# Attention columns from turned weights, adjacency loaded once, and exponentials turned by VectorE in a four-layer graph network

## The chip, the core and the metric

The kernel runs on one core of one Trainium2 chip. The metric is device time in microseconds (us) of the whole kernel. A core has five engines with queues of their own: TensorE (PE, matrix products and transposes into PSUM), VectorE (DVE), ScalarE (ACT), GpSimd (POOL) and SyncE (SP, which here only issues transfers). Transfers run on 16 DMA engines whatever queue issued them.

## The reference

128 graphs of 64 nodes with 256 features pass four layers. Each layer normalises its input, applies ReLU, and adds the layer's output to the input. `adj` is 128x64x64, integers 0 or 1.

```python
# layer 0: four heads (h) of 64 features (f)
Wh = (X @ W).reshape(B, N, H, F)
e_src = einsum('bnhf,hf->bnh', Wh, a_src)
e_dst = einsum('bjhf,hf->bjh', Wh, a_dst)
e = leaky_relu(e_src[:, :, None, :] + e_dst[:, None, :, :], 0.2)
alpha = softmax(where(A > 0, e, -1e9), axis=2)
out = elu(einsum('bijh,bjhf->bihf', alpha, Wh))
# layer 1: the same with one head; its vectors are a[:256] and a[256:]
# layer 2: relu(sum over relations r of (adj == r) @ ((x W + b_r) * sigmoid(x W Wg + bg_r)))
# layer 3: three steps of a GRU cell on aggr = A^T (h weight[i]) and h
```

Since `adj` holds 0 and 1 alone, of layer 2 only the relation 1 contributes. A flag computed on the chip sends other data to a general path, which these inputs don't take.

## The kernel before

**Tiling.** Two graphs fill the 128 partitions (a pair); four pairs are a group `g`, so there are 16 groups. Each group passes three layers of attention and relation and then three GRU steps. Everything is float32.

**Order.** The kernel body doesn't issue instructions; it notes them. `Plan.note` records each with its engine, an estimated cost, what it writes and reads, and the job it belongs to. `Plan.emit` (its last lines are around 525) then runs a list scheduler over the notes: `forward` places each instruction by an estimate of when its inputs, its engine and its buffers are free, `backward` derives due times from that, this is repeated `PASSES` times from a seed, and then a list of seeds `MOVES` shifts the due times of whole jobs. The order with which it ends is the order on every queue. Costs come from the function `cost` (line 575 and after): a transfer has a rate in bytes per ns by the tag of the tile that it fills. So a changed cost, an added instruction or another seed can reorder all five queues.

**Fillers.** In the first 115 us of that estimate, where TensorE is expected to idle, `emit` puts in products of a tile of ones, `warm` (line 1638), one for each 220 ns of the expected gap over 100 ns. Nobody reads their result.

**The first weights.** `attention_columns` appends to the weights `w0e` (256x256, held as 128x2x256) the columns W a_src and W a_dst of each head, so that one product gives Wh, e_src and e_dst together. VectorE makes them: `a_src` and `a_dst` are loaded onto all 128 partitions (`AB`), multiplied into the weights (`wa`) and summed by head. The same is done for `w1e`.

**Adjacency.** `load_group` loads `at`, integers, with four transfers of 32 KB; `edge_bounds` makes of it the bounds `m` (a huge number at an edge, a tiny one elsewhere, 0 in rows that have an edge and 1e-24 in rows that have none), turns them on TensorE into `mt`, and keeps the largest entry in `amax` for the flag. `load_edges` loads the same numbers as `ag` for the GRU, with another transfer, and as `eg`, turned otherwise, for layer 2. `before` (through `before_recurrence`) makes the 0/1 matrix `abd` out of `ag`.

**Exponentials.** `attention` writes the softmax's numerators without the sum of e_src and e_dst: exp(leaky(s+d)), divided by a factor of the row, is max(exp(d), exp(0.2 d) * exp(-0.8 s)). `fd` and `gd` are exp of the d half of `es`, per partition. exp(-0.8 s) has to lie along the free dimension, the same in all 64 partitions of a graph. For groups 0 and 1 (`g < AHEAD`) TensorE does that with a diagonal; for the 14 others ScalarE makes `fs`, TensorE transposes it, VectorE copies it out of PSUM to `fT`, one transfer writes it to DRAM (`row`) and two read it back into `t`, broadcast to 64 partitions each. Then three VectorE passes (`gd`, `fd`, `mt`) finish `t`, and 64x64 products on halves of the array (`aggregate_graphs`, line 841) use it.

**GRU.** `Recurrence.step` forms its matrix products in seven parts each (`sy`, `sz`). They are most of TensorE's instructions. Its transposes between steps go through DRAM (`tb`, `way`, `hnat`).

Almost all instructions carry line 549, that of the recording helper, so the profile tells them apart by the tiles' names.

Of the kernel before, what the change touches and what calls it, by code (L numbers as in the profile page):

```python
# [10 lines left out]
F32 = mybir.dt.float32  # L11
I32 = mybir.dt.int32
# [5 lines left out]
S = 32  # L18
# [9 lines left out]
NEG1 = -9000000000000000.0  # L28
ALPHA = 0.2
EPS = 1e-5  # L30
BIG, TINY = 3.0e38, 1.0e-24
BOUND = 6.25
NREL = 39
RC = 5
# [188 lines left out]
class Plan:  # L223
# [30 lines left out]
    def note(self, engine, call, cost, writes, reads, after=(), port=0.0, dma=False):  # L254
# [23 lines left out]
            b.ops.append(op)  # L278
        return op

    PASSES, SEED, SPREAD = 27, 39, 50.0
    MOVES = (
        10, 12, 18, 24, 27, 28, 58, 71, 83, 84, 89, 99, 118, 129, 136, 141, 144, 198, 214, 221, 266, 299, 322, 324,
        334, 341, 346, 390, 400, 412, 424, 434, 550, 559, 579, 611, 616, 682, 785, 808, 825, 869, 910, 1123, 1323,
        1710, 1729, 1754, 1784, 1908, 1924, 1933, 2133, 2158, 2174, 2755, 2883, 3921, 3988, 4026, 4270, 4596, 4876,
        4885, 5049, 5501, 5547, 5750, 5954, 6055, 6156, 6434, 6590, 7283, 7340, 7414, 7540, 7602, 7657, 7774, 7857,
        7930, 7942, 8201, 8457, 8683, 8685, 9083, 9436, 9811, 9967, 10320, 10820, 10999, 11484, 11701, 12627, 12696,
        12718, 12783, 12858, 12980, 13024, 13178, 13347, 13474, 14022, 14057, 14422, 14846, 16253, 16751, 16786,
        17194, 18227, 19571, 21611, 22526, 22951, 22990, 23107, 24055, 25299,
    )  # L290
    LEEWAY = {"PE": 100.0, "DVE": 100.0, "Activation": 100.0, "Pool": 100.0, "SP": 300.0, "-": 0.0}
    OVERLAP = {"DVE": 83.0, "Activation": 95.0, "Pool": 43.0}
# [210 lines left out]
    def emit(self):  # L503

        self.on = False
        self.link()
        best, self.random = None, Random(self.SEED)
        for _ in range(self.PASSES):
            ranks = [op.due for op in self.ops]
            end, order = self.forward()  # L510
            if best is None or end < best[0]:
                best = end, ranks, [op.start for op in self.ops]
            self.backward(end)
        end, ranks, starts = best
        jobs = list({id(op.job): op.job for op in self.ops}.values())
        for j in jobs:
            j.sum, j.count, j.shift = 0.0, 0, dict.fromkeys(self.RANKED, 0.0)
        for op, start in zip(self.ops, starts):
            op.job.sum, op.job.count = op.job.sum + start, op.job.count + 1
        for m in self.MOVES:  # L520
            self.move(m, end, jobs)
        for op, due in zip(self.ops, ranks):
            op.due = due + op.job.shift.get(op.engine, 0.0)
        end, order = self.forward()
        best = end, [(op, op.start, op.idle, op.places) for op in order]
        self.ends = best[0]
        for op, start, idle, places in best[1]:
            op.start = start
            if op.engine == "PE" and self.spare and start < 115.0 * 1e3:
                for _ in range(int((idle - 100.0) / 220.0)):  # L530
                    self.spare()
            for b, tag in places:
                b.pool.make(b, tag)
            op.call()
        self.ops = []
        return best[0]
# [46 lines left out]
def cost(engine, method, args, kwargs):  # L583
# [4 lines left out]
        return (m / 1.2 + 2.5) * (1 if method == "transpose" else 2)  # L588
    if engine == "sync" or method == "dma_start":
        to, of = args[:2]  # L590
        rate = {"way": 450.0, "fine": 220.0}.get(to.base.tag, 150.0) if isinstance(to, View) else 150.0
        if isinstance(of, View) and of.base.tag in ("way", "fine"):
            rate = 170.0 if of.base.tag == "way" else 125.0
        return n * to.shape[0] * 4 / rate
# [15 lines left out]
def kernel(  # L610
# [33 lines left out]
    xr = x.rearrange("b n d -> (b n) d").rearrange("(t q) d -> q t d", q=P)  # L644
    ar = adj.rearrange("b n m -> (b n) m").rearrange("(t q) m -> q t m", q=P)

    tr = adj.rearrange("(t r a) i j -> t a i r j", r=2, a=2)
    er = adj.rearrange("(t r a) j i -> t r j a i", r=2, a=2)
    outr = out.rearrange("b n d -> (b n) d").rearrange("(t q) d -> q t d", q=P)

# [7 lines left out]

    same = nc.kept(const, [P, P], F32, name="same")
    diag = nc.kept(const, [P, N], F32, name="diag")  # L660
    amax = nc.kept(const, [P, NG], F32, name="amax")
    flag = nc.kept(const, [1, 1], I32, name="flag")
    wc = nc.kept(const, [P, LAYERS, K, 3 * D], F32, name="wc")
    whh = nc.kept(const, [P, K, 3 * D], F32, name="whh")
# [554 lines left out]
    with ExitStack() as s1:  # L1219
# [47 lines left out]
        class Layer:  # L1267
# [2 lines left out]

            place = {"em": "hn", "dg": "hn", "tb": "hn", "land": "hn"}

            shared = {"hn": 3, "o": 2, "st": 4, "mv": 4, "var": 4, "rstd": 4, "nm": 4, "rec": 4, "fT": 1}

            def __init__(self, layer, pool, bufs):
                self.layer, self.pool, self.bufs = layer, pool, bufs
# [12 lines left out]
        W = [Layer(0, work, {"es": 2, "fd": 2, "gd": 2}), Layer(1, work, {}), Layer(2, work, {"u": 2})]  # L1289

        nc.begin("loads")
        AB = work.tile([P, 4, D], F32, name="AB", tag="o", bufs=2)
        for i, a in enumerate((a_src, a_dst)):
            nc.scalar.dma_start(AB[:, i, :], over_partitions(a, D))
        nc.scalar.dma_start(w0e[:, :, :D], rows(W0))
        AT, XG, AG, EG = [], [], [], []

        def load_group(g):
            nc.begin(("load", g))
            xg = work.tile([P, G, D], F32, name="xg", bufs=5)  # L1300
            n = 2 if g == 0 else G
            for p in range(0, G, n):
                nc.sync.dma_start(xg[:, p : p + n], xr[:, g * G + p : g * G + p + n, :])
            at = work.tile([P, G // 2, 2, N], I32, name="at", bufs=3)
            for a in range(2):
                for u in range(G // 2):
                    edges = tr[g * G // 2 + u, a]
                    nc.sync.dma_start(at[a * N : (a + 1) * N, u], edges)
            AT.append(at)
            XG.append(xg)  # L1310

        def load_edges(g):
            ag = work.tile([P, G, N], I32, name="ag", bufs=4)
            nc.sync.dma_start(ag, ar[:, g * G : (g + 1) * G, :])
            AG.append(ag)
            eg = work.tile([P, G, N], I32, name="eg", bufs=2)
            for r in range(2):
                for u in range(G // 2):
                    nc.sync.dma_start(eg[r * N : (r + 1) * N, 2 * u : 2 * u + 2], er[g * G // 2 + u, r])
            EG.append(eg)  # L1320
# [5 lines left out]
        load_group(1)  # L1326
        nc.begin("more loads")
        nc.sync.dma_start(w1e[:, :, :D], rows(W1))
        for i, a in enumerate((a1[:D], a1[D:])):
            nc.sync.dma_start(AB[:, 2 + i, :], over_partitions(a, D))  # L1330
        wn, gn = loaded(early, "wn", W_loop), loaded(early, "gn", Wg_loop)
        ihn, hhn = loaded(early, "ihn", w_ih), loaded(early, "hhn", w_hh)
        for i, b in enumerate((b_loop, bg_loop)):
# [16 lines left out]
        nc.vector.memset(mhalf, -0.5)  # L1350
        nc.vector.memset(eps, EPS)

        def attention_columns(w, heads, pieces):

            for i, ab in enumerate(pieces):
                wa = work.tile([P, K, D], F32, name="wa", tag="hn", bufs=3)
                nc.vector.tensor_tensor(wa, w[:, :, :D], ab[:, None, :].to_broadcast([P, K, D]), ALU.mult)
                nc.vector.tensor_reduce(
                    w[:, :, D + i * heads : D + (i + 1) * heads],
                    wa.rearrange("p k (h f) -> p k h f", h=heads), AX.X, ALU.add,  # L1360
                )

        wl = once.tile([P, K, 2 * D], F32, name="wl")

        def edge_bounds(g):


            at = AT[g]
            top = work.tile([P, G // 2, 2], F32, name="top")
            nc.vector.tensor_reduce(top, at, AX.X, ALU.max)  # L1370
            nc.vector.tensor_reduce(amax[:, g : g + 1], top, AX.XY, ALU.max)
            nc.vector.tensor_scalar(top, top, 0.0, TINY, op0=ALU.is_le, op1=ALU.mult)
            m = work.tile([P, G // 2, 2, N], F32, name="m", bufs=1)
            nc.vector.tensor_scalar(m, at, 0.0, BIG, op0=ALU.is_gt, op1=ALU.mult)
            nc.vector.tensor_tensor(m, m, top[:, :, :, None].to_broadcast([P, G // 2, 2, N]), ALU.max)
            pt = psum.tile([P, T], F32, name="tp")
            for u in range(G // 2):
                nc.tensor.transpose(pt[:, u * P : (u + 1) * P], m[:, u].rearrange("p g j -> p (g j)"), ident)
# [4 lines left out]
        def attention(g, p0, n, layer, heads, we, pool):  # L1383
# [31 lines left out]
                    )  # L1415
            else:

                fs = pool.tile([P, n, heads], F32, name="fs")
                nc.scalar.activation(fs, es[:, :, :heads], AF.Exp, scale=ALPHA - 1.0)
                pt = psum.tile([P, T], F32, name="tp")  # L1420
                nc.tensor.transpose(pt[:nh, :P], fs.rearrange("p g h -> p (g h)"), ident)
                fT = pool.tile([nh, P], F32, name="fT")
                nc.vector.tensor_copy(fT, pt[:nh, :P])
                row = dram.tile([2, nh * N], F32, name=f"row{layer}")
                nc.sync.dma_start(row.rearrange("a (c i) -> c a i", i=N), fT.rearrange("c (a i) -> c a i", i=N))
                for half in range(2):
                    nc.sync.dma_start(
                        t[half * N : (half + 1) * N].rearrange("p c i -> p (c i)"),
                        row[half : half + 1, :].to_broadcast([N, nh * N]),
                    )  # L1430
            flat = lambda d, c: d.rearrange("p g h -> p (g h)")[:, c, None].to_broadcast([P, len(range(nh)[c]), N])
            m = 2 if heads > 1 else n
# [8 lines left out]
            elu_add(pool, src, o, nc.vector if g < 1 else nc.gpsimd, g >= AHEAD)  # L1441

        def first_weights():
            attention_columns(w0e, H, (AB[:, 0, :], AB[:, 1, :]))
            attention_columns(w1e, 1, (AB[:, 2, :], AB[:, 3, :]))

        def later_weights(prep):
            relational_weights(prep, psum, wl, wn, gn, 0.5)
# [79 lines left out]
        def before(g):  # L1528
            ABD[g] = work.tile([P, G, N], F32, name="abd")
            by_dma = dram if g >= AHEAD else None  # L1530
            START[g] = before_recurrence(W[3], psum, XG[g], AG[g], ABD[g], by_dma, g in PLAIN)

        def recur(g):
            return Recurrence(
# [321 lines left out]
```

## Time and profile before

| | us |
|---|---|
| median of 3 runs | 1317.81 |
| lowest, highest | 1317.18, 1320.26 |
| profiled execution | 1316.05 |
| its span, first to last instruction | 1314.2 |
| granted TensorE clock | 0.998 |

The page gives for each engine its busy time, its share of the span and its instructions; then 40 slices of the span; then the DMA queues, the chain of work that ended last, the costliest groups and the transfers. On TensorE a matrix product of float32 appears as two records, a transpose as one, and their ends are modelled. Its chain of work goes through TensorE for 85% of the span:

```profile
PE 85%; DVE 5%; ACT 5%; POOL 2%; issue 1%; DMA 1%; SPq 0%; ACTq 0%; DVEq 0%; POOLq 0%
```

Transfers that the change touches, with KB each and the median us from issue to landing:

```profile
t<-row SPq DMA_DIRECT2D x28, 256.0 KB, 4.1
at<-in_adj_dram SPq DMA_DIRECT2D x64, 32.0 KB, 2.5
...
ag<-in_adj_dram SPq DMA_DIRECT2D x16, 128.0 KB, 2.8
t<-row SPq DMA_DIRECT2D x28, 64.0 KB, 2.6
```

### The profile page before, as it was taken

The page shows a single profiled execution, that of the slowest core. Times are in us where ns is not written, and L with a number is a line of the kernel's source. Part 1 is how long each engine was busy: PE and PEld are TensorE (multiplying, and loading weights), DVE is VectorE, ACT ScalarE, POOL GpSimd, SP SyncE. Part 2 cuts the span into 40 slices and gives each one's busy share as a digit, 9 for nine tenths or more (in the row PEclk, how much of TensorE's full clock was granted, in tenths as well). Part 3 has the DMA queues.
Part 4 walks back from the last instruction along what each step waited for, and adds up shares of the span by engine and source line. Part 5 has one row for each costly group of instructions (what it writes and reads, how often), then busy time and mean ns, then how long its engine had stood idle before and what let it go on. Part 6 is the DMA issues. An engine that isn't in the chain of part 4 may idle for free.

```text
span 1314.2 us, 27889 instructions
## 1 busy us (share of the span) xinstructions
PE 1298.9 (99%) x9837; PEld 1030.0 (78%) x9837; DVE 1058.3 (81%) x2562; ACT 856.6 (65%) x2173; POOL 694.3 (53%) x845
## 2 busy tenths in 40 slices
PE   9999999999999999999999999999999999999997
PEld 8667887878787777878778787877878788778885
DVE  6878667978879798897968889796887979786666
ACT  5867765666776676667766666776666667645543
POOL 2745744646555545546535564654556447445453
PEclk9999999999999999999999999999999999999999
DMA  7232122335334343443434344334334423142222
GB/s 229 66 101 58 53 85 89 110 121 161 110 117 143 115 138 94 144 122 116 126 118 142 92 150 120 104 122 132 113 104 143 132 86 129 38 129 65 65 65 68
DMA packets 132782, 144.94 MB, mean 110 GB/s; under 512 B 43417, under 2 KB 117913, under 8 KB 132633
## 3 DMA queue, kind: packets, MB, share of 16 engines
q1 hardware_dynamic: 132072, 142.54, 35.8%
q8 instruction: 80, 1.31, 0.4%
q10 hardware_dynamic: 560, 0.52, 0.1%
q14 instruction: 70, 0.57, 0.1%
HBM read 81.01 MB, written 61.49 MB: 108 GB/s over the span
## 4 chain that ended last, share of the span: by engine, by line
PE 85%; DVE 5%; ACT 5%; POOL 2%; issue 1%; DMA 1%; SPq 0%; ACTq 0%; DVEq 0%; POOLq 0%
PE sy L549 34%; PE sz L549 25%; PE mm L549 15%; PE mm L841 3%; PE tp L841 3%; ACT hn L549 2%; DVE hT L549 2%; PE sz L1638 1%; PE tp L549 1%; DVE t L549 1%; ACT hT L549 1%; PE tq L841 1%; DVE r L549 1%; POOL rstd L549 1%; DVE st L549 1%
## 5 line engine op out<-in xcount | busy, mean ns | idle before, releaser
L549 POOL TENSOR_TENSOR r<-hT,hT 128x256 f32<-128x256 f32 x192 | 156.2, 820 | 274.9 <-ACT hT L549 273.6
L549 DVE SCALAR_TENSOR_TENSOR hT<-r,hT 128x256 f32<-128x256 f32 (+1 forms) x290 | 182.4, 633 | 26.8 <-ACT r L549 24.5
L549 PE MATMUL sy<-hS,wsum 128*128 128x256 f32 x576 | 172.4, 383 | 1.2 <-ACT r L549 0.7
L549 PE MATMUL sy<-aS,wsum 128*128 128x256 f32 x576 | 172.4, 382 | 0.0
L549 PE MATMUL sz<-hS,whh 128*128 128x256 f32 x576 | 171.4, 383 | 0.6 <-DVE z L549 0.6
L549 PE MATMUL sz<-aS,wc 128*128 128x256 f32 x576 | 167.0, 383 | 0.8 <-DVE hT L549 0.8
L549 DVE TENSOR_TENSOR hT<-hT,sz 128x256 f32<-128x256 f32 x288 | 118.2, 410 | 39.5 <-PE sz L549 32.9
L549 ACT ACTIVATE hT<-hT,bi 128x256 f32<-128x256 f32 x192 | 95.7, 505 | 61.9 <-DVE hT L549 60.8
L549 POOL TENSOR_TENSOR aS<-aT 128x256 f32<-128x256 f32 x96 | 82.5, 859 | 94.0 <-ACT aT L549 94.0
L549 PEld LDWEIGHTS sy<-hS,wsum 128*128 128x128 f32 x576 | 106.8, 190 | 30.4 <-issue 9.4
L549 PEld LDWEIGHTS sy<-aS,wsum 128*128 128x128 f32 x576 | 107.6, 190 | 21.1 <-issue 4.2
L549 PEld LDWEIGHTS sz<-hS,whh 128*128 128x128 f32 x576 | 106.4, 190 | 22.4 <-issue 5.2
L549 PEld LDWEIGHTS sz<-aS,wc 128*128 128x128 f32 x576 | 106.9, 190 | 17.8 <-DVE hT L549 1.2
L549 ACT ACTIVATE hn<-xg,nm,rstd 128x256 f32<-128x256 f32 x200 | 108.0, 592 | 19.6 <-POOL nm L549 18.3
L549 ACT ACTIVATE hT<-sy,bh 128x256 f32<-128x256 f32 x192 | 90.2, 470 | 45.6 <-PE sy L549 42.4
L549 POOL TENSOR_TENSOR rstd<-var,mhalf 128x4 f32<-128x4 f32 (+1 forms) x70 | 78.1, 1115 | 77.0 <-ACT var L549 76.8
L549 PE MATMUL mm<-wl,hT 128*128 128x512 f32 x248 | 118.6, 594 | 0.0
L549 ACT COPY z<-sy 128x256 f32<-128x256 f32 x192 | 70.4, 367 | 64.9 <-PE sy L549 63.7
L549 DVE TENSOR_TENSOR hT<-hT,sy 128x256 f32<-128x256 f32 x192 | 79.3, 413 | 36.3 <-PE sy L549 34.1
L549 DVE BATCH_NORM_STATS2 st<-xg 128x6 f32<-128x256 f32 x256 | 96.3, 408 | 8.2 <-POOL xg L549 4.8
L549 DVE TENSOR_TENSOR z<-sz,z 128x256 f32<-128x256 f32 x192 | 79.5, 415 | 28.7 <-PE sz L549 27.2
L549 POOL TENSOR_TENSOR hS<-hT 128x256 f32<-128x256 f32 x96 | 80.0, 834 | 38.1 <-DMA hT<-way 15.2
(207 smaller groups left out, 3212.6 us busy)
## 6 DMA issues: line engine op xcount, KB each, us to landing
way<-tb SPq DMA_DIRECT2D x59, 512.0 KB, 2.7
hnat<-way SPq DMA_DIRECT2D x184, 128.0 KB, 3.0
way<-hn SPq DMA_DIRECT2D x42, 512.0 KB, 3.0
hn<-way SPq DMA_DIRECT2D x168, 128.0 KB, 3.1
xg<-in_x_dram SPq DMA_DIRECT2D x15, 512.0 KB, 4.4
out_dram<-xg SPq DMA_DIRECT2D x15, 512.0 KB, 2.9
t<-row SPq DMA_DIRECT2D x28, 256.0 KB, 4.1
hT<-way SPq DMA_DIRECT2D x52, 128.0 KB, 2.8
```

Of the source, the lines that this page charges most:

```text
L549: return do(*[real(a) for a in args], **{k: real(v) for k, v in kwargs.items()})
L841: nc.nc.tensor.matmul(*[real(x) for x in product], start=True, stop=True)
L1638: nc.spare = lambda: psum.spare and nc.nc.tensor.matmul(pause, warm, warm, start=True, stop=True)
```

## The change

1. **Attention columns on TensorE.** The vectors are loaded element by element onto partitions as `ab` (three transfers on ACT's queue, behind `w0e`). VectorE places them in a block-diagonal `e0` (and `e1`), TensorE transposes the weights (4 transposes each), ScalarE copies them to `wT`, TensorE multiplies `wT` with `e0`, and ScalarE copies the result into the weights' last columns. The multiplications and reductions on VectorE go.
2. **Adjacency once.** `at` is one transfer for each group, in six buffers, and serves `edge_bounds` and `abd`; `ag` goes. In `edge_bounds` one `scalar_tensor_tensor` takes the place of two passes, and `amax` keeps each row's largest entry directly (64 columns instead of 16). The huge number becomes 1e29.
3. **Exponentials turned by VectorE.** For the 14 later groups `fs` is 128x32, exp(-0.8 x) of both halves of `es` (in layer 1 eight columns, GpSimd clears the rest once a group); VectorE turns its four blocks of 32x32 in place; four transfers, one for each block, write them to `row`; two read the s half of it into `t`, in runs of one pair instead of one run.
4. **The listing.** Rates of transfers in `cost` (190 for `t`, 290 for most loads, was 150), 40 passes, another seed and other moves, and in the first 12 us of the estimate a filler for each 280 ns of a gap instead of 220.

```diff
-    PASSES, SEED, SPREAD = 27, 39, 50.0
+    PASSES, SEED, SPREAD = 40, 35, 50.0
...
-                for _ in range(int((idle - 100.0) / 220.0)):
+                for _ in range(int((idle - 100.0) / (280.0 if start < 12e3 else 220.0))):
                     self.spare()
...
-        rate = {"way": 450.0, "fine": 220.0}.get(to.base.tag, 150.0) if isinstance(to, View) else 150.0
+        tag = to.base.tag if isinstance(to, View) else None
+        rate = {"way": 450.0, "fine": 220.0, "t0": 190.0, "t1": 190.0}.get(tag, 150.0 if tag in (None, "at", "eg", "o", "row0", "row1") else 290.0)
...
-            at = work.tile([P, G // 2, 2, N], I32, name="at", bufs=3)
-            for a in range(2):
-                for u in range(G // 2):
-                    edges = tr[g * G // 2 + u, a]
-                    nc.sync.dma_start(at[a * N : (a + 1) * N, u], edges)
+            at = work.tile([P, G, N], I32, name="at", bufs=6)
+            nc.sync.dma_start(at, ar[:, g * G : (g + 1) * G, :])
...
-            ag = work.tile([P, G, N], I32, name="ag", bufs=4)
-            nc.sync.dma_start(ag, ar[:, g * G : (g + 1) * G, :])
...
-        def attention_columns(w, heads, pieces):
-            for i, ab in enumerate(pieces):
-                wa = work.tile([P, K, D], F32, name="wa", tag="hn", bufs=3)
-                nc.vector.tensor_tensor(wa, w[:, :, :D], ab[:, None, :].to_broadcast([P, K, D]), ALU.mult)
-                nc.vector.tensor_reduce(
-                    w[:, :, D + i * heads : D + (i + 1) * heads],
-                    wa.rearrange("p k (h f) -> p k h f", h=heads), AX.X, ALU.add,
-                )
+        def attention_columns(w, heads, ends):
+            wT = work.tile([P, K, D], F32, name="wT", tag="hn", bufs=3)
+            for c in range(K):
+                pt = psum.tile([P, T], F32, name="tp")
+                for k in range(K):
+                    nc.tensor.transpose(pt[:, k * P : (k + 1) * P], w[:, k, c * P : (c + 1) * P], ident)
+                nc.scalar.copy(wT[:, c], pt[:, :D])
+            n = 2 * heads
+            pm = psum.tile([P, K, n], F32, name="mm")
+            def products():
+                for k in range(K):
+                    for c in range(K):
+                        nc.nc.tensor.matmul(
+                            real(pm)[:, k], real(wT)[:, c, k * P : (k + 1) * P], real(ends)[:, c, :n],
+                            start=(c == 0), stop=(c == K - 1),
+                        )
+            nc.note("PE", products, 880.0, [pm], [wT, ends])
+            nc.scalar.copy(w[:, :, D:], pm)
...
-            nc.vector.tensor_scalar(m, at, 0.0, BIG, op0=ALU.is_gt, op1=ALU.mult)
-            nc.vector.tensor_tensor(m, m, top[:, :, :, None].to_broadcast([P, G // 2, 2, N]), ALU.max)
+            nc.vector.scalar_tensor_tensor(
+                m.rearrange("p u r j -> p (u r) j"), AT[g], BIG,
+                top.rearrange("p u r -> p (u r)")[:, :, None].to_broadcast([P, G, N]), op0=ALU.mult, op1=ALU.max,
+            )
...
-                nc.scalar.activation(fs, es[:, :, :heads], AF.Exp, scale=ALPHA - 1.0)
-                pt = psum.tile([P, T], F32, name="tp")
-                nc.tensor.transpose(pt[:nh, :P], fs.rearrange("p g h -> p (g h)"), ident)
-                fT = pool.tile([nh, P], F32, name="fT")
-                nc.vector.tensor_copy(fT, pt[:nh, :P])
-                nc.sync.dma_start(row.rearrange("a (c i) -> c a i", i=N), fT.rearrange("c (a i) -> c a i", i=N))
+                nc.scalar.activation(fs[:, :used], es.rearrange("p g h -> p (g h)"), AF.Exp, scale=ALPHA - 1.0)
+                fT = pool.tile([P, S], F32, name="fT")
+                nc.vector.transpose(fT, fs)
+                row = dram.tile([2, S // (2 * heads), 2, heads * N], F32, name=f"row{layer}")
+                for q in range(P // S):
+                    nc.sync.dma_start(
+                        row[q // 2].rearrange("x s (h i) -> (x s h) i", i=N)[:, q % 2 * S : (q % 2 + 1) * S],
+                        fT[q * S : (q + 1) * S],
+                    )
...
+            for i in range(2):
+                for h in range(H):
+                    c, half = h // 2, slice(h % 2 * N, (h % 2 + 1) * N)
+                    nc.vector.tensor_copy(e0[half, c, i * H + h : i * H + h + 1], ab[half, i, c : c + 1])
```

## The prediction

> **What bounds the kernel now.** I read the page's busy shares and its slices first, then the busy time by stretches, then TensorE's waits, and last the chain of waits and TensorE's timeline of the first 20 us.
>
> ```profile
> PE 1298.9 (99%) x9837; PEld 1030.0 (78%) x9837; DVE 1058.3 (81%) x2562; ACT 856.6 (65%) x2173; POOL 694.3 (53%) x845
> ...
> PEclk9999999999999999999999999999999999999999
> ```
> ```profile
> 0.00:15.00 15.00, 13.94 (x106) 13.94 (x107) 7.82 (x30) 4.68 (x11) 2.66 (x14) 1.00 0.78 211
> 15.00:120.00 105.00, 102.95 (x753) 70.77 (x752) 86.62 (x260) 81.58 (x257) 58.69 (x91) 1.00 0.37 100
> 120.00:1290.00 1170.00, 1167.28 (x8915) 933.75 (x8915) 951.05 (x2246) 763.23 (x1889) 626.82 (x736) 1.00 0.36 110
> 1290.00:1315.00 25.00, 14.77 (x68) 11.55 (x66) 12.77 (x29) 7.12 (x16) 6.12 (x6) 0.88 0.27 88
> ```
>
> A busy PE can be a PE whose matmuls overlap, so 99% alone proves little. The rate supports it: a matmul of 256 columns is two records and the timeline repeats it every 0.43 us (0.216 us a record), and between 120 and 1290 us only 2.7 us of 1170 lie open. No other engine is over 82% there. So from about 120 us on the time is the sum of TensorE's work: a microsecond less of it is a microsecond, and work taken from VectorE is worth nothing by itself. The waits agree; the longest of TensorE's own are these, and all eleven entries sum to 8.7 us, about half of it in the last 20 us.
>
> ```profile
> PE tp L549 <- DVE hT L549: 1.9, 3, 1.2
> PE sy L549 <- DVE hT L549: 1.4, 1, 1.4
> PE sz L1638 <- DVE mhalf L549: 1.1, 1, 1.1
> ```
>
> The first 120 us look as full and are not: part of what fills them is the filler of line 1638, a product whose result nobody reads.
>
> ```profile
> L1638 PE MATMUL sz<-warm 128*128 128x128 f32 x168 | 24.5, 294 | 1.1 <-DVE mhalf L549 1.1
> ...
> L549 PE MATMUL tp<-ident,fs 128*16 128x128 f32 (+1 forms) x28 | 7.6, 273 | 0.0
> ```
> ```profile
> 1.06 11.23 PE L1638 MATMUL sz<-warm 128*128 128x128 f32 x80 [1.06 <-DVE mhalf L549]
> 12.13 0.60 PE L549 MATMUL tp<-ident,hn 128*128 128x128 f32 x4
> 12.57 2.62 PE L1638 MATMUL sz<-warm 128*128 128x128 f32 x22
> 15.02 0.61 PE L549 MATMUL mm<-w0e,hT 128*128 128x264 f32 x2
> ```
>
> A filler is two records. The same timeline cut at 7 us has 35 records in 6.21 us, so the other 45 take 5.02 us: 0.112 us a record, 0.224 a filler; the early ones come at about half that rate. ScalarE had written the first normalised pair (`hn`, 6.88 us, 1.09 long) at 7.97, yet its transposes start at 12.13, behind fillers. The fillers that should bridge a wait are themselves the wait, and the chain of waits names them for 11.23 and 2.46 us.
>
> **The change part by part.** The order of TensorE's instructions is known from the program; durations are from the trace.
>
> (a) *The first products.* TensorE's new order: 17 fillers, 4 transposes of `w0e`, 9 fillers, 4 products with `e0`, 4 transposes of `hn`, 2 fillers, 4 of `hn`, then `mm<-w0e`. The 34 records end near 7.0 us (the 35th ended at 7.27, and one lasts 0.275); 4 transposes at 0.109 (four take 0.44 on the chain): 7.4; 18 records: 9.45. The 8-column products are 8 records: 0.03 us each by the only narrow row (`mm<-wq`, one weight column), 0.112 by the filler, which like them loads 128 weight columns. I take the filler, 0.9 in all: 10.35. Then 0.44 + 0.45 + 0.44: **11.7 us against 15.02, -3.3 us**. Is anything later than that? The `ab` loads come after `w0e` on ACT's queue, issued by about 2.8 us; `bi`, the same form with 4-byte runs, landed after 2.4, the old `AB` after 4.8, so 5.2 to 7.6, and the nine small copies on DVE (0.15 to 0.17 each by `wq`, 1.4) give 9.0: before 9.45. ScalarE does two `wT` copies (0.37) at about 7.4 to 8.1 ahead of `hn`, then four `hn` (2.2) to 10.3: just in time for the second pair's transposes at 11.1. Moreover four DVE passes of 0.68 and four reductions of 0.69, 5.5 us, leave VectorE in the first 18 us.
>
> Here two rules of the Trainium skill speak against the change. "TensorE: Matmul & The Clock Gate", Part 1, says that about 3.4 us without work set the array back to half rate until about 3.4 us of work have passed. 84 fillers become 48 (-36, 8.1 us); by the rule each gap opened to that length costs about 1.7 us. By the rows: 26 of the first fillers remain in two blocks around the first transposes, later gaps are served by waits of at most 1.1 us ahead of it, so I take 0. "DMA: Bandwidth & Descriptors", Specifications, wants 512 B a run; the change has 4-byte, 128-byte and 256-byte runs. Its row here: `hT<-tb` moves 32 KB in 128-byte runs in 2.0 us, `at` 32 KB in 256-byte runs in 2.5, no slower than larger ones (2.6 to 4.1). I take the rows: no charge.
>
> (b) *15 to 120 us.* 33 fillers become 20: 13 x 0.224 = 2.9 us less idle in the listing. In their place stand the columns of `w1e`: 4 transposes (0.44) and 8 narrow records (0.9 as above). Net **-1.6 us**. From below: +1.3 if real gaps appear where fillers were; from above -4, since SP now issues the second group's `xg` as its third transfer instead of its tenth (7.34 us before; 6 adjacency issues of about 0.63 fewer for two groups, 3.8 us).
>
> (c) *The transposes of `fs`.* 28 leave TensorE at 0.109 each: **-3.05 us**, all but two after 120 us, where it counts. Instead ACT's `Exp` handles both halves of `es` (32 or 8 columns, row 0.22), VectorE turns 128x32 (its 128x512 takes 0.69; bounded below by its smallest rows, 0.15) instead of a copy of 0.27, GpSimd clears a strip 14 times. Four stores replace one. `row<-fT` issues in 0.30 us now, so the fourth is 0.9 us behind (0.6 an issue, as `hT<-tb`: 1.8). Behind these in SP's queue stand the two loads of `t`, and the `way` loads next to them. Not on TensorE, but see the rival.
>
> (d) *Adjacency once.* Per group 5 DMAs become 1 (SP issues 897 instead of 879, with the extra stores); edge_bounds loses a 128x256 pass (0.28) and a reduction of 0.15: 16 x 0.43 = 6.9 us of VectorE beside a full TensorE: 0. So too `abd` from `at`, already resident.
>
> (e) *The order.* New seeds and durations turn the whole listing. Counted out of it: runs of half-array products 133 to 134; entering and leaving one costs about 0.2 us together: +0.2. The last 70 matmuls stand in the same order, so the tail of 25 us is taken unchanged.
>
> Sum: -3.3 - 1.6 - 3.05 + 0.2 = -7.8 us. The profiled execution took 1316.05 us (span 1314.2, 1.85 around it), 1.76 under the median of 1317.81. Span 1314.2 - 7.8 = 1306.4, execution 1308.3, median **1310.0 us**.
>
> **Rivals.** *The lead is lost in the ramp.* Between 20 and 88 us ScalarE, VectorE and TensorE are each some 80% busy and wait for one another in turns (the chain there mixes all three with GpSimd), and ScalarE gains four copies of 0.37. If that mesh sets when TensorE fills, (a) and (b) vanish: only -3.05 + 0.2 remains: 1315.0. For it: the mixed chain. Against: the load of VectorE, its first members and the second group's data all come earlier.
>
> *The earlier data carry further.* If (b) reaches its -4 and the gain in (a) is joined by 2 us of waits in the ramp: -3.3 - 4 - 2 - 2.85 = -12.2: 1305.6. Against: the listing still plans 20 fillers there.
>
> *The row of exponentials comes late (slower).* Before, the path from `fs` to VectorE's first use of `t` in the first layer takes about 5.9 us (286.44 to 292.36 in the timeline), and `t` lands in 4.1 us at 64 partitions of one run each; VectorE takes it up almost on landing. If four issues, 1 KB runs and a blocked SP queue delay it by 1.5 us, and TensorE has nothing else listed, 14 groups cost 21 us: 1310.0 + 21 = 1331. It decides from 7.8/14 = 0.56 us of TensorE waiting a group. For it: that tight path. Against: VectorE waited for `t<-row` only twice, 1.4 us in all; a transpose that queued on TensorE and a copy out of PSUM leave the path (1.2 us from `fs` to `fT` there); and work of other groups stands beside it.
>
> *The change doesn't do what it says* in one part: the refit moves transfers wrongly, so that TensorE's order meets loads that aren't there. Its size is that of the last rival's onset, 0 to +8 us: 1310 to 1318.
>
> **How the numbers follow.** Forecast 0.61, its own range 1306.5 to 1313.5 (the ends of (b), the narrow products at 0.03 instead of 0.112 us, and 1 us of middle waits either way). Lead lost 0.15. Further 0.11. Refit wrong, about no change 0.06. Row late 0.07. A measurement of this kernel can tell about 0.3%, 4 us, from no change: "faster" means under 1313.9. Faster: the forecast nearly whole (0.60), the further one (0.11), a third of the lead-lost case (0.05): 0.76. Same: 0.15. Slower: 0.09, the late row and some of the refit. The range leaves out the late row and the far end of the further case: 1303.5 to 1316.5.
>
> **What would show it.** Right: `mm<-w0e` starts at 11 to 12.5 us; `sz<-warm` has about 96 records; `tp<-ident,fs` is gone; the 120 to 1290 stretch is still open by less than 4 us; TensorE's waits are still under 10 us in all. (a) is wrong if the narrow products wait for `ab`; (b) if the stretch from 15 to 120 us shows more open time than 2.05 us with fewer fillers; (c) if TensorE waits for `t` of VectorE, or VectorE for `t<-row`, by more than 8 us. A granted clock under 1.00 in the first stretches, or records at double spacing after 10 us, would make the clock rule right.

## The result, and the profile after

| | before | after |
|---|---|---|
| median of 12 runs, us | 1317.61 | 1312.44 |
| lowest, highest, us | 1316.40, 1320.26 | 1307.17, 1316.84 |
| profiled execution, its span, us | 1316.05, 1314.2 | 1311.0, 1309.2 |

The ratio is 0.9958, with a 95% interval of 0.9947 to 0.9969: the changed kernel is faster by about 5.2 us (0.4%), where 7.8 had been forecast. Its runs spread over 9.7 us, those of before over 3.9; why they spread so isn't shown.

The page of the changed kernel, engines' busy time and the clock's slices:

```profile
PE 1288.8 (98%) x9761; PEld 1024.4 (78%) x9761; DVE 1052.5 (80%) x2532; ACT 857.7 (66%) x2179; POOL 700.3 (53%) x859
...
PEclk9999999999999999999999999999999999999998
```

TensorE has 76 records fewer: 72 of fillers and 28 transposes less, 8 transposes and 16 narrow products more. TensorE's busy time fell by 10.1 us, more than the 7.8 of the forecast; the span fell by only 5.0. The stretches show where the rest went (columns as before: length, then TensorE's busy time, then the others', and the granted clock behind the five engines):

```profile
0.00:15.00 15.00, 13.94 (x97) 13.32 (x98) 7.98 (x46) 9.36 (x32) 5.32 (x19) 1.00 0.93 282
15.00:120.00 105.00, 103.44 (x748) 72.58 (x747) 87.00 (x247) 83.83 (x257) 58.55 (x91) 1.00 0.31 88
120.00:1290.00 1170.00, 1162.65 (x8884) 932.53 (x8883) 946.91 (x2217) 760.07 (x1882) 631.22 (x745) 1.00 0.36 109
1290.00:1315.00 25.00, 8.79 (x38) 5.96 (x36) 10.61 (x23) 4.39 (x9) 5.23 (x5) 0.80 0.16 47
```

The stretch from 15 to 120 us, from which fillers were taken, has less open time than before (1.56 us, was 2.05). The middle, which the prediction took as unchanged, has 7.35 us open where it had 2.72. TensorE's waits (total, how often, longest) have grown accordingly; the second line of before, 1.4 us for `hT`, is now 2.8, and two entries of over a microsecond are new:

```profile
PE sy L550 <- DVE hT L550: 2.8, 3, 1.7
PE tp L550 <- DVE hT L550: 2.0, 4, 0.9
PE sy L550 <- ACT z L550: 1.5, 1, 1.5
PE mm L842 <- issue: 1.2, 1, 1.2
PE sz L1664 <- DVE warm L1662: 1.1, 1, 1.1
```

The fillers' group and TensorE's timeline from the start show the first part of the change (start, length, instruction, and in brackets the idle time before it):

```profile
L1664 PE MATMUL sz<-warm 128*128 128x128 f32 x96 | 14.8, 298 | 1.1 <-DVE warm L1662 1.1
```
```profile
1.06 5.43 PE L1664 MATMUL sz<-warm 128*128 128x128 f32 x34 [1.06 <-DVE warm L1662]
6.33 0.60 PE L550 MATMUL tp<-ident,w0e 128*128 128x128 f32 x4
6.76 2.17 PE L1664 MATMUL sz<-warm 128*128 128x128 f32 x18
8.77 0.96 PE L1366 MATMUL mm<-e,wT 128*128 128x8 f32 x8
9.59 0.64 PE L550 MATMUL tp<-ident,hn 128*128 128x128 f32 x4
10.06 0.61 PE L1664 MATMUL sz<-warm 128*128 128x128 f32 x4
10.50 0.63 PE L550 MATMUL tp<-ident,hn 128*128 128x128 f32 x4
10.97 1.95 PE L550 MATMUL mm<-w0e,hT 128*128 128x264 f32 x8
```

The order is the predicted one, no bracket stands before the narrow products `mm<-e,wT`, and `mm<-w0e` starts at 10.97 us instead of 15.02.

**Where the middle's time went.** The three longest gaps of TensorE there are at 386, 526 and 600 us. This is the timeline of all engines at the first of them:

```profile
383.75 2.80 POOL L550 TENSOR_TENSOR xg<-xg,hn 128x1024 f32<-128x1024 f32 x1
...
384.60 2.50 DVE L550 SCALAR_TENSOR_TENSOR hT<-r,hT 128x512 f32<-128x512 f32 x1
...
385.83 0.59 PE L550 MATMUL sz<-hS,whh 128*128 128x256 f32 x2
...
387.20 0.37 ACT L550 COPY r<-sy 128x256 f32<-128x256 f32 x1 [1.99 <-DVE hT L550]
...
387.47 0.38 ACT L550 COPY z<-sy 128x256 f32<-128x256 f32 x1
...
387.90 0.48 PE L550 MATMUL sy<-hS,wsum 128*128 128x256 f32 x1 [1.48 <-ACT z L550]
```

The wait's own label names ScalarE's `z`. Followed back, `z` stood behind the copy `r`, which waited 1.99 us for VectorE's `hT`. That instruction has two operands in SBUF. Where one of its kind and size meets nothing on GpSimd it takes 0.68 us (median of 25), here 2.50. It began while GpSimd's long addition (the residual `xg`) was running and ended half a microsecond after it. The gap at 526 us has the same shape: an addition of 2.43 us from 524.16, an `hT` of 128x256 held from 524.29 for 2.58 us (0.42 alone, median of 107), TensorE idle for 1.66. At 219 us it is 2.08 us for `hT` and 0.83 for TensorE. The gap at 600 us is another: there VectorE waited 2.35 us for the row of exponentials, `t<-row`, and TensorE 1.2.

Such held instructions aren't new. Counting VectorE's instructions of two operands that overlap one of the long additions and last 2 us or more, before has 11 and after 6. In before they cost TensorE one wait over a microsecond, the 1.4 us shown there, at 1221 us. What has changed is where they fall in the listing, and how much TensorE still has to do while one lasts.

### The profile page after: what moved, and what is told of

It reads as the page before. It is cut to its first block, busy times and chain, and to the rows that moved or that the text cites. A ratio compares the mean times of both kernels' runs of the same rounds, so it can differ in the third digit from the quotient of the medians.

```text
span 1309.2 us, 27708 instructions
## 1 busy us (share of the span) xinstructions
PE 1288.8 (98%) x9761; PEld 1024.4 (78%) x9761; DVE 1052.5 (80%) x2532; ACT 857.7 (66%) x2179; POOL 700.3 (53%) x859
## 4 chain that ended last, share of the span: by engine, by line
PE 86%; DVE 6%; POOL 3%; ACT 3%; issue 1%; DMA 1%; SPq 0%; DVEq 0%; ACTq 0%; POOLq 0%
PE sy L550 35%; PE sz L550 26%; PE mm L550 16%; PE mm L842 3%; PE tp L842 3%; DVE hT L550 2%; DVE t L550 1%; PE tp L550 1%; POOL rstd L550 1%; ACT hn L550 1%; PE sz L1664 1%; PE tq L842 1%; POOL xg L550 1%; DVE r L550 1%; DMA t<-row 1%
## 5 line engine op out<-in xcount | busy, mean ns | idle before, releaser
L550 DVE SCALAR_TENSOR_TENSOR hT<-r,hT 128x256 f32<-128x256 f32 (+1 forms) x290 | 186.4, 647 | 27.1 <-ACT r L550 24.7
L550 POOL TENSOR_TENSOR aS<-aT 128x256 f32<-128x256 f32 x96 | 79.0, 823 | 81.6 <-ACT aT L550 78.8
```

What stands on the lines that cost most here:

```text
L550: return do(*[real(a) for a in args], **{k: real(v) for k, v in kwargs.items()})
```

## Experiments

All ratios are to the kernel before, with 95% intervals. "Mid open" is TensorE's open time between 120 and 1290 us in the profiled execution (2.72 before, 7.35 after).

**1. Is a lead at the start carried to the end?** The rival "lost in the ramp" said no. Two kernels move only fillers; the order of everything else is kept on all queues. In the first, before has fewer of them:

```diff
-                for _ in range(int((idle - 100.0) / 220.0)):
+                for _ in range(int((idle - 100.0) / (440.0 if start < 20e3 else 220.0))):
```

> The kernel before with 28 of its 51 first fillers taken out (blocks of 40 and 11 become 20 and 5), every other instruction in the same order on every queue. Theory 'the lead carries' (fillers hold back the first product, and what is gained there is kept to the end): the first w0e product starts at about 10 us instead of 15.0, and the time falls by about 5 us, to 1312 to 1313. Rival 'lost in the ramp' (the mesh of engines between 20 and 120 us sets when TensorE fills): the product starts as early, but the time stays within 1.5 us of 1317.6. Clock rule: the wider gaps bring half-rate records after 6 us and the time does not fall.

1314.82 us (1312.48 to 1317.41), ratio 0.9976 (0.9969 to 0.9982). `mm<-w0e` starts at 9.90 us, 5.1 earlier:

```profile
9.90 0.68 PE L549 MATMUL mm<-w0e,hT 128*128 128x264 f32 x2 [0.38 <-ACT hn L549]
```

The same products of before then stand 5.2 us earlier at 20, at 112 and at 258 us: the ramp takes nothing. At the end 3.1 us of it are left in the medians. In the profiled execution (1316.32 us, one of the slower ones of this kernel) TensorE's last record is only 1.1 us earlier and the last store takes 1.5 us longer; mid open is 6.34.

This run says more than the rival asked. It keeps the old columns, the old adjacency and the old exponentials, takes out 28 fillers in one line, and has 3.1 of the 5.2 us of the whole change. Its first product starts 1.1 us before that of after (10.97), with columns that VectorE still makes: the lead at the start comes from fewer fillers, and columns made on TensorE are not needed for it.

One toll, in the timeline of this kernel:

```profile
684.10 2.42 POOL L549 TENSOR_TENSOR xg<-xg,hnat 128x1024 f32<-128x1024 f32 x1
...
684.24 3.37 DVE L549 SCALAR_TENSOR_TENSOR hn<-hn,o 128x1024 f32<-128x1024 f32 x1
...
687.69 2.35 POOL L549 TENSOR_TENSOR xg<-xg,hn 128x1024 f32<-128x1024 f32 x1 [1.16 <-DVE hn L549]
687.86 2.46 DVE L549 SCALAR_TENSOR_TENSOR hT<-r,hT 128x256 f32<-128x256 f32 x1
687.99 0.30 PEld L549 LDWEIGHTS sy<-aS,wsum 128*128 128x128 f32 x2 [1.94 <-DVE hT L549]
687.99 0.48 PE L549 MATMUL sy<-aS,wsum 128*128 128x256 f32 x1 [1.52 <-DVE hT L549]
```

In before the same `hn<-hn,o` takes 1.74 us, since there the addition begins after it has ended. Same program, same order, shifted by 5 us: the two fell together, and TensorE lost 1.5 us. The ramp is not where a lead is lost; the middle is.

In the second, after has more of them:

```diff
-                for _ in range(int((idle - 100.0) / (280.0 if start < 12e3 else 220.0))):
+                for _ in range(int((idle - 100.0) / (120.0 if start < 12e3 else 220.0))):
```

> The changed kernel with its first three blocks of fillers at 39, 22 and 5 instead of 17, 9 and 2, all else in the same order. Theory 'the lead carries': 38 fillers of 0.224 us push the first w0e product from 11.0 to about 19.5 us and the time from 1312.4 to about 1321. Rival 'lost in the ramp': the product starts as late, but the time rises by at most 3 us.

1320.55 us (1318.59 to 1324.76), ratio 1.0031 (1.0022 to 1.0039). `mm<-w0e` starts at 20.94 us in the profiled execution, 10.0 later, and the median is 8.1 later. The 38 fillers at 0.224 us account for 8.5 of the 10.0; the rest is the slower pace of the first records, which differs from execution to execution (see (a) below). So nearly all of the delay arrives.

**2. Is TensorE's work still the time?** Each of the 32 transposes of `m` is done four times over, 96 more at 0.109 us, 10.5 us in all; the order is kept.

```diff
-                nc.tensor.transpose(pt[:, u * P : (u + 1) * P], m[:, u].rearrange("p g j -> p (g j)"), ident)
+                def four(to=to, of=of):
+                    for _ in range(4):
+                        nc.nc.tensor.transpose(real(to), real(of), real(ident))
```

> The changed kernel with each of the 32 transposes of m done four times over, the order unchanged: 96 x 0.109 = 10.5 us more of TensorE's work, spread over the groups. Theory 'a microsecond of TensorE's work is a microsecond': 1312.4 + 10.5 = about 1323. Rival 'other engines share the bound': clearly less, say 1315 to 1319, because waits shrink as work is added.

1320.43 us (1317.5 to 1322.97), ratio 1.0020 (1.0014 to 1.0027): 8.0 us above after for 10.5 us of work. The two intervals leave 6.5 to 9.9 us. So a microsecond of TensorE is about three quarters of one here. Turned round, 28 transposes fewer would be some 2.3 us and not 3.05, though this experiment adds work and takes none away.

**3. Does GpSimd's addition hold VectorE?** The 43 long additions are issued as two of half the length, in the same place.

```diff
+    def add_in_two(to, plus):
+        def emit():
...
+            for s in (slice(0, n), slice(n, 2 * n)):
+                nc.nc.gpsimd.tensor_tensor(a[:, s], a[:, s], b[:, s], ALU.add)
```

> The changed kernel with GpSimd's additions of 128x1024 (xg<-xg,hn and xg<-xg,hnat, about 2.4 us each) issued as two of 128x512, the order unchanged. Theory 'port': VectorE instructions that start behind such an addition last up to 2.9 us instead of 0.6, and three of TensorE's longest waits (at 219, 386 and 526 us) stand behind one; in two parts the hold is half as long, TensorE's waits between 120 and 1290 us fall by 1.5 to 3 us and the time to about 1310. Rival 'late rows of exponentials': the waits come from t<-row and stay, the time is within 1 us of 1312.4, or above it since GpSimd's additions take a little longer.

1311.42 us (1310.59 to 1312.69), ratio 0.9955 (0.9942 to 0.9969). The same place as above, in its timeline (the two halves on one line, 3.40 us together):

```profile
383.59 3.40 POOL L871 TENSOR_TENSOR xg<-xg,hn 128x512 f32<-128x512 f32 x2
...
384.44 1.42 DVE L550 SCALAR_TENSOR_TENSOR hT<-r,hT 128x512 f32<-128x512 f32 x1
...
386.67 0.70 PE L550 MATMUL sy<-hS,wsum 128*128 128x256 f32 x2 [0.41 <-ACT z L550]
```

`hT` begins as before, behind a running addition, and ends after 1.42 us instead of 2.50, 0.55 us after the first half (at 385.31) and before the second (at 386.99); TensorE waits 0.41 instead of 1.48. The hold is shown, and that it ends with the instruction that holds. The gap at 219 us went too; the one at 526 stayed (1.65), where two instructions of VectorE in a row met one half each. Yet mid open is 7.72: other waits took the place, and the median is only 1.0 us below after, less than such runs can tell.

A second kernel took the additions of the attention's end away from GpSimd, to VectorE at the same place of the listing:

```diff
+            nc.note(
+                "Pool", lambda: nc.nc.vector.tensor_tensor(real(src), real(src), real(em), ALU.add),
...
```

> The changed kernel with the attention layers' additions xg<-xg,hn on VectorE (about 1.2 us each for 128x1024, 0.7 for 128x512) at the same place of the order instead of on GpSimd (2.4 us); the 15 of the GRU's end stay on GpSimd. Theory 'port': most of the holds vanish, VectorE's additions cost it about 35 us that it has idle: waits of TensorE between 120 and 1290 us fall by 2 to 3 us, about 1310. Rival: on a VectorE that is 81% busy the additions delay what TensorE waits for as much as the holds did, 1312 to 1316.

1329.11 us (1326.56 to 1330.83), ratio 1.0090 (1.0075 to 1.0106), mid open 15.9. That is 16.7 us above after, and no theory had it. Here an addition of 128x1024 stands in VectorE's own queue for 1.2 us (its median). A likely reason is that everything behind it waits always, not only when it meets another; but the listing wasn't fitted to this either, and the run doesn't separate the two.

**4. Are the parts worth something alone?** Two kernels mix the old and the new. One is after with the old path of the exponentials:

```diff
-                nc.vector.transpose(fT, fs)
...
+                nc.tensor.transpose(pt[:nh, :P], fs.rearrange("p g h -> p (g h)"), ident)
+                fT = pool.tile([nh, P], F32, name="fT")
+                nc.vector.tensor_copy(fT, pt[:nh, :P])
```

> The changed kernel with the exponentials turned as before (TensorE transposes fs, one store), all else of the change kept; the scheduler lists the program anew with the changed kernel's seeds. Theory (28 transposes of 0.109 us come back on a full TensorE; the late rows cost it only the 1.4 us wait at 600 us): +3.05 - 1.4, about 1314, plus what seeds fitted to another program lose (0 to 4 us). Rival 'the row comes late': the four stores cost TensorE 3 us or more, so the time is at or below 1312.4.

1343.67 us, ratio 1.0202 (1.0188 to 1.0216), mid open 17.2. The other is before with only the new listing:

```diff
-    PASSES, SEED, SPREAD = 27, 39, 50.0
+    PASSES, SEED, SPREAD = 40, 35, 50.0
...
+        rate = {"way": 450.0, "fine": 220.0, "t0": 190.0, "t1": 190.0}.get(tag, 150.0 if tag in (None, "at", "eg", "o", "row0", "row1") else 290.0)
```

> The kernel before with the listing of the change alone (rates, passes, seed, moves, fillers of 280 ns): columns, adjacency and exponentials as before. Theory 'the parts bring it': first block of 28 fillers instead of 40, the first w0e product near 12 us, a lead of 2 to 3 us at most, of which unfitted seeds may take all: 1315 to 1320. Rival 'the listing brings it': 1312 to 1314 with nothing else changed.

1342.87 us, ratio 1.0186 (1.0172 to 1.0199), mid open 12.7. Both lie far above what was expected. Neither says what its part is worth: seeds and moves that were found for one set of instructions give another set just some order, and that costs 25 to 31 us. So the parts were compared without any fit, both kernels with the moves left out:

```diff
-        for m in self.MOVES:
-            self.move(m, end, jobs)
```

> The kernel before with the list of moves left out of its scheduler, all else as before; to be read against e10. Theory 'the fit of the listing to its own program is worth 20 us or more' (e5 and e6 lost 25 to 31): about 1340 to 1350. Rival 'unfitted seeds are worse than none': 1320 to 1330.

> The changed kernel with the list of moves left out. Theory 'the parts bring some 5 us, by TensorE's earlier first product and 28 transposes fewer, whatever the listing': 3 to 10 us faster than e9. Rival 'the gain is the fit': the difference to e9 is under 3 us or of the other sign.

Before so: 1325.01 us (1324.62 to 1325.86), ratio 1.0058 (1.0043 to 1.0072). After so: 1324.65 us (1322.35 to 1327.03), ratio 1.0062 (1.0047 to 1.0077). They are equal within the 3 us that so few runs tell apart, although the second begins its first products at 11.33 us against 16.58 and has 28 transposes fewer; its mid open is 10.5 against 7.47. The fit is worth 7.4 us to before and 12.2 to after, less than the 20 expected, and seeds of another program are dearer than none. One order of each is a single draw, so this doesn't show that the parts are worth nothing; it shows that without a fitted listing their gain can go whole into waits. What each part is worth alone stays open, but for the fillers of experiment 1: taking one back and fitting the listing anew wasn't tried. Nor was before fitted anew with its own parts, so a share of the gain could come from the new search for seeds.

**5. Can it be better?** Three kernels combine what was learned: fewer fillers (11, 6 and 1 in the first 12 us, none later), with and without the halved additions, and then two of the four stores of `row` issued from ScalarE's queue.

```diff
-            if op.engine == "PE" and self.spare and start < 115.0 * 1e3:
-                for _ in range(int((idle - 100.0) / (280.0 if start < 12e3 else 220.0))):
+            if op.engine == "PE" and self.spare and start < 12.0 * 1e3:
+                for _ in range(int((idle - 100.0) / 400.0)):
```

> e4 (additions in two parts) with the first three blocks of fillers at 11, 6 and 1 instead of 17, 9 and 2 and none after them (20 fewer). Theory: the first w0e product is now held by the landing of ab (5.7 us from issue) and by ScalarE, so it starts at most 1 us earlier than 11.0; of the 20 later fillers a few stood in the way: 1309.5 to 1311. Clock rule: without the later fillers some gaps of the ramp bring records at double spacing and the time is above 1312.

> The changed kernel with the fillers of e8 (11, 6, 1, then none) and the additions whole as in the change: which part of e8's 2.9 us is the fillers'. Theory 'fillers': about 1310.5, of which e4's split (1.0 us by its median) is the rest. Theory 'additions in two parts': about 1312, as the change.

With halved additions 1309.52 us (1308.89 to 1311.91), ratio 0.9941 (0.9928 to 0.9955); with whole ones 1312.61 (1310.28 to 1313.87), ratio 0.9962 (0.9949 to 0.9975). Fewer fillers still give nothing by themselves: 1312.61 against 1312.44. Halving the additions beside that lowers the median by 3.1 us, with mid open 7.59 against 9.36; the intervals overlap a little, and without the fewer fillers it was 1.0 us. The fewer fillers also show what is late next at the start: with whole additions the narrow products wait 1.3 us for `e`, that is for `ab` (in the kernel with halves, whose first records were slower, they wait 0.4 us, put down to ScalarE's `hn`).

```diff
+                    if q % 2 == 0:
+                        nc.sync.dma_start(to, of)
+                    else:
...
+                            "SP", lambda to=to, of=of: nc.nc.scalar.dma_start(real(to), real(of)),
```

> e8 with two of the four stores of each row of exponentials issued from ScalarE's queue instead of SP's. Rival of the prediction 'the row comes late': the loads of t are issued about 0.8 us earlier, the 1.4 us wait of TensorE at 597 us goes, and so do most of VectorE's 8.6 us of waits for t<-row: 1308 or less. Against it: ScalarE pays some 0.5 us for each of 56 issues between its own instructions, which TensorE waits for in places: 1310 to 1313.

1307.8 us (1306.96 to 1313.3), ratio 0.9937 (0.9922 to 0.9951), the best of all: 4.6 us below after, 1.7 below the one without it, which the runs can't tell from nothing. The two traces differ at the gap of 600 us, as the expectation said. VectorE's timeline there, first the kernel with one queue, then this one:

```profile
595.83 0.59 DVE L550 TENSOR_TENSOR t<-t,gd 128x256 f32<-128x256 f32 x1 [2.73 <-DMA t<-row]
596.46 0.83 DVE L550 TENSOR_TENSOR t<-t,fd 128x256 f32<-128x256 f32 x1
597.33 0.83 DVE L550 TENSOR_TENSOR t<-t,mt 128x256 f32<-128x256 f32 x1
```
```profile
594.88 0.42 DVE L550 TENSOR_TENSOR t<-t,gd 128x256 f32<-128x256 f32 x1 [1.37 <-DMA t<-row]
595.33 0.42 DVE L550 TENSOR_TENSOR t<-t,fd 128x256 f32<-128x256 f32 x1
595.79 0.42 DVE L550 TENSOR_TENSOR t<-t,mt 128x256 f32<-128x256 f32 x1
```

The row comes 0.95 us earlier, and the three passes then miss GpSimd's short additions, which had doubled two of them (0.83 for 0.42). TensorE's 1.2 us of waiting at this place are gone, and mid open falls from 7.59 to 4.60. The general claim of the expectation wasn't met: over all 28 rows the first load of `t` is issued 5.2 us after `fs` is ready (median), against 4.9 with one queue, and VectorE still waits 9.4 us for `t<-row`, against 11.2. So one row was gained, and the second queue isn't shown to be the cause of the rest.

## Why the prediction was right, and where its size was off

The likeliest case happened: 1312.4 lies in that case's own range, and TensorE's work fell by each of the terms (a) to (c). What was off is the term that was taken as nothing, the middle. That the result still fell into the range is in part luck: TensorE's busy time fell by 10.1 us, 2.2 more than (a), (b) and (c) together had it, and so paid for half of what the middle lost.

| term (profiled execution) | forecast | measured |
|---|---|---|
| (a) first products | -3.3 | -4.05 |
| (b) 13 fillers out, columns of `w1e` in | -1.6 | -1.65 |
| (c) 28 transposes of `fs` | -3.05 | -3.05 |
| (e) half-array runs | +0.2 | not told apart |
| open, 15 to 120 us | 0 | -0.5 |
| open, 120 to 1290 us | 0 | +4.6 |
| open, last 25 us; last store | 0 | -0.2; +1.2 |
| busy time not assigned to a term | | -1.4 |
| span | -7.8 | -5.0 |

(b) and (c) under "measured" are records counted in the trace times their spacing (0.112 and 0.109 us), and (a) is read off the timeline. Of the 1.4 us, 0.44 belong to (a): in before only one of the two pairs of `hn` had been turned when `mm<-w0e` began at 15.02 us, and its other four transposes follow at 15.47; in the new order all eight stand ahead of the product. The prediction compared 11.7 with 15.02 and so left these four out.

**(a)** The mechanism was right, and the figure 0.75 us too small; `mm<-w0e` came just ahead of the 11 to 12.5 us that were named. The first 34 records, 17 fillers, took 5.3 us instead of 5.9, since records at double spacing gave way sooner. That is no effect of the change. In the eleven profiled executions that begin with 34 such records, these take 5.3 to 6.8 us up to the next instruction: 5.9 in before, and 6.4 in the kernel with the transposes done four times, whose first block is this:

```profile
1.06 6.60 PE L1670 MATMUL sz<-warm 128*128 128x128 f32 x34 [1.06 <-DVE warm L1668]
```

So most of the 0.75 us is chance. The narrow products took 0.82 us against 0.9, so the filler was the right row to take for them. `ab` landed 4.8 to 5.9 us after its issue, later than the 2.4 to 4.8 estimated, and VectorE had `e` at 8.65, still before 8.77. That margin was 0.1 us, which experiment 5 made visible. By experiment 1 the whole lead could be had without these columns.

**(b)** Right. The rival "earlier data carry further" didn't happen: the stretch has 0.5 us of open time less, not 2 and more.

**(c)** The transposes went. The sign that was set for it being wrong, VectorE waiting over 8 us for `t<-row`, was just met. Here are these waits in before and in after (total, how often, longest):

```profile
DVE t L549 <- DMA t<-row: 1.4, 2, 1.1
```
```profile
DVE t L550 <- DMA t<-row: 8.6, 10, 2.3
```

Only one of these waits reached TensorE as a long one, 1.2 us at 600 us. So the rival "the row comes late" was real in kind. The path did get longer, by more issues and a store that lands in 1.8 us (1.3 before): `fT` is ready 0.4 us after `fs` instead of 1.6, and yet the first load of `t` is issued 5.0 us after `fs` instead of 3.3 (medians of 28). That delay of 1.7 us is the 1.5 that the rival asked for. What it had wrong is its other half, "and TensorE has nothing else listed": it needed 0.56 us of TensorE in each of 14 groups to decide; it was 1.2 us in one.

**(d), (e)** VectorE's busy time fell from 1058.3 to 1052.5 us and nothing follows from it, as said.

**The middle.** The step that failed is "1 us of middle waits either way", drawn from the 2.7 us that lay open before. That figure was no property of the kernel: it belonged to one fitted order. A shift changes which VectorE instructions meet GpSimd's additions and which rows come in time, and experiment 1 shows it with no change but fillers (2.72 to 6.34 us). Of the 4.6 us that the middle lost, the gaps behind held instructions at 219, 386 and 526 us make 4.0 (0.83 + 1.48 + 1.66) against 1.4 before, the late row 1.2, and a turn of `hn` at 639 us, which waited for the result of GpSimd's `xg`, 1.0; small gaps make up the difference. The test "still open by less than 4 us" was therefore failed, and "TensorE's waits under 10 us" too (some 13).

Of the rivals, "lost in the ramp" falls by experiment 1. "The refit moves transfers wrongly" falls in after itself: none of TensorE's waits there names a transfer, the one long gap that goes back to one is the row's 1.2 us, and the moves are worth 12.2 us to it. The sum took it for granted that the new order would fit as well as the old one; the difference of what the two fits are worth, 4.8 us, is nearly as large as the whole gain.

**The clock and the short runs.** Both choices of the prediction held, the second only just. The adjacency of a group in one transfer of 256-byte runs lands in 2.6 us (`ag`, as large, took 2.8), the `t` rows in 4.0 and 2.7 (4.1 and 2.6); `ab`, 1 to 2 KB in 4-byte runs, is the one that came late. With 48 fillers instead of 84, and with 18 in experiment 5, the granted clock is 1.00 in the first three stretches. But the rule that was weighed is real, and two experiments show it. The granted clock (the number behind the five engines) in the unfitted after and in before with the new listing:

```profile
1098.00:1101.00 3.00, 3.00 (x8) 2.44 (x9) 3.00 (x11) 0.54 (x2) 2.62 (x4) 0.52 0.32 135
```
```profile
49.00:53.00 4.00, 3.95 (x15) 3.40 (x16) 3.18 (x19) 2.20 (x8) 0.60 (x2) 0.57 0.72 221
```

The first follows waits of 1.92 and 0.65 us with one matmul between them, the second a wait of 4.45 us. "TensorE: Matmul & The Clock Gate", Part 1, asks for about 3.4 us of idle; the second agrees, the first fell short of it in each single wait and was still slowed. In after no wait is over 1.7 us, and the granted clock stays at 1.00 up to the last 25 us: taking 0 was right.

## What to carry to other kernels

Where one engine is nearly full under a fitted list order, sum the removed work and then expect a toll: of a lead of 5.1 us 3.1 reached the end, of 10.5 us of added work 8.0, of the forecast's 7.8 us 5.2. It is no fixed factor, since a delay of 8.5 us arrived nearly whole (8.1). Before building parts that clear the way for an engine, try the cheapest edit that clears it: here one line on fillers had 3.1 of the 5.2 us. Look for the toll where two engines share something that the listing's costs know only roughly, and follow a wait's label back past the engine that it names. And compare a part with the whole only where both have a listing of their own: seeds fitted to other instructions cost 25 to 31 us, five times what the whole change is worth.

## What the runs showed of the hardware

- VectorE with two operands in SBUF stands still while a long GpSimd addition runs. In after, no such instruction lies wholly inside one of the long additions; six that began early in one ended after it, with 2.1 to 2.7 us in place of 0.42 to 0.69. The 79 passes of 128x256 with an operand in PSUM that do lie inside kept their 0.38 to 0.43 us, and so did the transposes and statistics of one operand. One pass with a single operand didn't: `abd<-at` began 0.23 us into an addition at 166 us and took 2.27 us, where its median is 0.28. "SBUF — State Buffer", "SBUF: two separate sides", says the same: the port is held for the whole instruction and not shared. The 1.42 us with halved additions agree.
- The first matmul records come at double spacing (0.213 us) for 2.9 to 6.1 us from the first one on, over the fourteen profiles, while the granted clock in the rows already reads 1.00.
- The last store of the output, from the start of TensorE's last record to the end of the span, took between 5.8 and 7.7 us over all profiles, with no change to it. It makes 1.2 us of the difference between the two profiles.
